# Late nodes of an attention layer as five interleaved generators, with edge pieces at 1.5 a step

## The chip, the core and the metric

The kernel runs on one core of one Trainium2 chip. The metric is the device time of the whole program in microseconds. The core has a tensor engine (PE, whose weight loads the profile shows apart as PEld), a vector engine (DVE), a scalar engine (ACT), GpSimd (POOL), and a queue of its own for plain DMAs (SP). Each engine works through its own list of instructions in order, and semaphores join the lists.

## What is computed

The reference takes 6250 nodes with 128 features and 100000 edges, sorted by destination, and runs four residual blocks of graph layers over them: a mean over neighbours, a product over edges with a radial filter, three layers of neighbour means, and three layers of graph attention. Only the last block matters here. Cut to what is computed, one of its three layers is this:

```python
h = x @ W
al = leaky_relu(h[src] @ a_src + h[dst] @ a_dst + edge_attr @ We @ a_edge, 0.2)   # edges and self loops
ex = exp(al - segment_max(al, dst)[dst])
out = segment_sum(h[src] * ex, dst) / (segment_sum(ex, dst) + 1e-16) + bias
x = batch_norm(leaky_relu(out, 0.01))
```

## The kernel before

The nodes lie in an array of 125 partitions by 50. Each attention layer (`attention_split`) treats them in two parts, in the function `split_edges`, whose instructions are most of the layer's time.

**Early nodes** belong to the first 64 partitions of that array: 3200 nodes, five groups of 128 by 5. For them the gather and the sum are matrix products. A loop of 160 steps, 32 to a group, makes one-hot matrices in each step (`ready`, for the step two ahead: `hot_n` on DVE and ACT, `hot_c` on ACT, from `half_n` and `hot` that SP has loaded), multiplies them on PE into `cnt` (four products), and copies `cnt` to `m` on ACT (L1706). Eight steps make a unit `m`; the next eight steps multiply it with the features on PE (`product`, tile `o`, seven products a step). In the first 128 steps the next group's coefficients are prepared beside that: `source_terms` in the first 20 steps of a group (PE into `x_ps`, DVE from it), and `softmax` in the other 12.

**Late nodes** are the other 3050, 122 partitions by 25 in the code (`R2`, `T2`). Their edges lie in 125 runs of 400. The generator `late` walks all the runs at once, in 50 chunks of 8 edges. A chunk has 8 gathers on POOL into `rows` (three buffers), a short softmax on DVE (`al`, `top`, `ex`) with one exponential on ACT, one product, and 8 dependent accumulations on DVE into `acc` (two buffers), which SP stores to `late_hist` in DRAM. It is cut into four pieces by `yield`. After 200 pieces, `late_fix` repairs sums that cross from one run into another, in seven further pieces, and scatters the result into `late_hist`. Then `late_tail` reads the final sums of the nodes from there, in five blocks of five columns. A block loads the nodes' own rows (`own_h`, by SP), gathers the sums (`agg`, five on POOL), runs through three empty pieces, computes scale factors (`sc`), scales `own_h` on ACT, joins the two on DVE (`stt`, L82), transposes on PE (`tp`), adds the bias on ACT (`z_l`), and gives the activation, the statistics and the copy to `y_t`. `late_tail` runs one block after the other, with eight pieces to a block.

The loop over steps decides how many pieces of `late` each step takes, and this is the order on each engine: at the end of `split_edges` every PE, DVE and ACT instruction is tied to the one recorded before it. POOL and SP are not tied; they run ahead as far as their buffers allow. Before the loop about ten pieces are already done. In the loop:

```python
            while done < min(200, 10 + (step + 1) * 1.38):
                next(edges_late)
                done += 1
            if step > 140:
                for _ in islice(edges_late, 3):
                    pass
```

So the edges end at step 137, the repair begins at step 141 with three pieces a step, and the late nodes follow up to step 157. In a step the pieces stand behind the `m` copy, and ahead of the next step's `cnt`. The helpers `tt`, `ts`, `stt`, `transpose`, `gather`, `scatter` and `bulk` issue one operation each (`bulk` two DMAs); the profile shows their lines (L73, L77, L82, L156, L55, L68, L51 and L52).

Of the kernel before, what the change touches and what calls it, by code (L numbers as in the profile page):

```python
# [39 lines left out]
def kernel(ctx: ExitStack, tc: tile.TileContext, a: dict, out: bass.AP):  # L40
# [7 lines left out]
    def bulk(dst, src, eng=None):  # L48

        eng = eng or nc.sync  # L50
        eng.dma_start(dst[0:PS], src[0:PS])  # L51
        eng.dma_start(dst[PS:], src[PS:])  # L52

    def gather(dst, table, idx):
        nc.gpsimd.indirect_dma_start(  # L55
            out=dst, out_offset=None, in_=table,
            in_offset=bass.IndirectOffsetOnAxis(ap=idx, axis=0))
# [14 lines left out]
    def tt(o, x, y, op):  # L72
        nc.vector.tensor_tensor(o, x, y, op)  # L73

    def ts(o, x, s1, op0, s2=None, op1=None):
        if op1 is None:
            nc.vector.tensor_scalar(o, x, s1, None, op0=op0)  # L77
        else:
            nc.vector.tensor_scalar(o, x, s1, s2, op0=op0, op1=op1)  # L79
# [1058 lines left out]
    def late_nodes(ap, t0, n, width):  # L1138
        return bass.AP(tensor=ap.tensor, offset=ap.offset + (N1 + t0) * width, ap=[[T2 * width, R2], [1, n * width]])
# [311 lines left out]
    def split_edges(lt, i, table, own_d, bias, parts, early_d, late_d, ade, tails, stats, stats_l, pool, ps):  # L1451
# [104 lines left out]
        def late():  # L1556

            NB = 8  # L1560
            top = pool.tile([P, C2 + 1], F32, name="top", bufs=1)
            nc.vector.memset(top[:, 0:1], 0.0)
            prev = None
            for c0 in range(0, C2, NB):
                all_rows = pool.tile([128, NB, W], F32, name="rows", bufs=3)
                for j in range(NB):
                    gather(all_rows[:, j, :], table, lt.src[:, c0 + j:c0 + j + 1])
                rows = all_rows[:P]
                al = pool.tile([P, NB], F32, name="al")
                ex = pool.tile([P, 2, NB], F32, name="ex")  # L1570
                now, before = top[:, c0 + 1:c0 + NB + 1], top[:, c0:c0 + NB]
                tt(al, rows[:, :, AL], ade[:, c0:c0 + NB], OP.add)
                stt(al, al, 0.2, al, OP.mult, OP.max)
                nc.vector.tensor_tensor_scan(now, lt.pen[:, c0:c0 + NB], al, top[:, c0:c0 + 1], op0=OP.add, op1=OP.max)
                tt(ex[:, 0, :], al, now, OP.subtract)
                tt(ex[:, 1, :], before, now, OP.subtract)
                stt(ex[:, 1, :], ex[:, 1, :], 0.0, lt.pen[:, c0:c0 + NB], OP.min, OP.add)
                nc.scalar.activation(ex, ex, AF.Exp)
                yield
                acc = pool.tile([P, NB, W], F32, name="acc")  # L1580
                tt(rows, rows, ex[:, 0, :, None].to_broadcast([P, NB, W]), OP.mult)
                yield
                for j in range(NB):
                    if c0 + j == 0:
                        nc.vector.tensor_copy(acc[:, 0, :], rows[:, 0, :])
                    else:
                        stt(acc[:, j, :], prev, ex[:, 1, j:j + 1], rows[:, j, :], OP.mult, OP.add)
                    prev = acc[:, j, :]
                    if j == NB // 2 - 1:
                        yield  # L1590
                nc.scalar.activation(acc[:, :, AL], now, AF.Copy)
                bulk(bass.AP(tensor=late_hist.tensor, offset=late_hist.offset + c0 * W, ap=[[C2 * W, P], [1, NB * W]]),
                     acc.rearrange("p c f -> p (c f)"))
                yield
            nc.scalar.activation(tails, prev, AF.Copy)
            yield from late_fix(lt, tails, pool, ps)
            yield from late_tail(lt, table, late_d, lt.e_self[i], bias, stats_l, pool, ps)

        def first_terms(al_s):

# [89 lines left out]
        for step in range(steps):  # L1690
            g, s = divmod(step, 32)
            unit, u = divmod(step, 8)
            if s == 0 and g < GP - 1:
                al_s = pool.tile([128, 128], F32, name="al_s")
                terms, soft = source_terms(g + 1, al_s), softmax(g + 1, al_s)
            if u == 0:
                m = pool.tile([128, T, NW, 32], F32, name="m")
            cnt = ps.tile([128, 4, 256], F32, name="cnt", bufs=2)
            hot_n, hot_c = hots.pop(0)
            for w in range(4):  # L1700
                nc.tensor.matmul(cnt[:P, w, :T * NW], lhsT=hot_c[:, w, :P], rhs=hot_n[:, w, :], start=True, stop=True)  # L1701
            if step + 2 < steps:
                hots.append(ready(step + 2))
            for _ in islice(before, 7):
                pass
            nc.scalar.activation(m[:P, :, :, u * 4:u * 4 + 4].rearrange("p l k q -> p k l q"),  # L1706
                                 cnt[:P, :, :T * NW].rearrange("p w (k l) -> p k l w", k=NW), AF.Copy)
            if g < GP - 1:
                if s < 20:
                    for _ in islice(terms, 2 if s % 5 < 3 else 1):  # L1710
                        pass
                else:
                    next(soft, None)
            while done < min(200, 10 + (step + 1) * 1.38):
                next(edges_late)
                done += 1
            if step > 140:
                for _ in islice(edges_late, 3):
                    pass
            if u == 7:  # L1720
                for _ in before:
                    pass
                before = product(unit, m)
# [45 lines left out]
        nc.vector.tensor_copy(fixed[:, AL:AL + 1], mx[:, 1:2])  # L1769
        scatter(late_hist, lt.fix, fixed, P * C2)  # L1770

    def late_tail(lt, table, late_d, e_self, bias, stats_l, pool, ps):

        NK = 5
        for t0 in range(0, T2, NK):
            all_agg = pool.tile([128, NK, W], F32, name="agg", tag="acc")
            agg = all_agg[:R2]
            own_h = pool.tile([R2, NK, W], F32, name="own_h", tag="rows", bufs=3)
            bulk(own_h.rearrange("p t f -> p (t f)"), late_nodes(table, t0, NK, W))
            for j in range(NK):  # L1780
                gather(all_agg[:, j, :], late_hist, lt.end[:, t0 + j:t0 + j + 1])
            for _ in range(3):
                yield
            sc = pool.tile([R2, 6, NK], F32, name="sc")
            own, m = sc[:, 0, :], sc[:, 1, :]
            tt(own, own_h[:, :, AL], late_d[:, t0:t0 + NK], OP.add)
            ts(own, own, e_self[:R2], OP.add)
            stt(own, own, 0.2, own, OP.mult, OP.max)
            tt(m, agg[:, :, AL], own, OP.max)
            tt(sc[:, 2, :], agg[:, :, AL], m, OP.subtract)  # L1790
            tt(sc[:, 3, :], own, m, OP.subtract)
            nc.scalar.activation(sc[:, 2:4, :], sc[:, 2:4, :], AF.Exp)
            yield
            den = sc[:, 4, :]
            tt(den, agg[:, :, ONE], sc[:, 2, :], OP.mult)
            tt(den, den, sc[:, 3, :], OP.add)
            ts(den, den, 1e-16, OP.add)
            nc.vector.reciprocal(den, den)
            tt(sc[:, 2, :], sc[:, 2, :], den, OP.mult)
            tt(sc[:, 3, :], sc[:, 3, :], den, OP.mult)  # L1800
            for j in range(NK):
                nc.scalar.activation(own_h[:, j, :D], own_h[:, j, :D], AF.Copy, scale=sc[:, 3, j:j + 1])  # L1802
            yield
            for j in range(NK):
                stt(agg[:, j, :D], agg[:, j, :D], sc[:, 2, j:j + 1], own_h[:, j, :D], OP.mult, OP.add)
            z = pool.tile([128, NK, R2], F32, name="z_l", tag="wide", bufs=1)
            for j0 in range(0, NK, 2):
                n = min(2, NK - j0)
                tp = ps.tile([128, 2, R2], F32, name="tp", tag="x_ps")
                for j in range(n):  # L1810
                    transpose(tp[:, j, :], agg[:, j0 + j, :D])
                nc.scalar.activation(z[:, j0:j0 + n, :], tp[:, :n, :], AF.Identity, bias=bias, scale=1.0)  # L1812
                if j0 < 4:
                    yield
            stt(z, z, 0.01, z, OP.mult, OP.max)
            for j in range(NK):
                nc.vector.bn_stats(stats_l[:, t0 + j, :], z[:, j, :])
            nc.scalar.activation(lt.y_t.rearrange("f (h c) p -> f c h p", h=2)[:, t0:t0 + NK, :, P1:],
                                 z.rearrange("f c (p h) -> f c h p", h=2), AF.Copy)
            yield  # L1820

    def attention_layers(h_sb, arm=""):
        with tc.tile_pool(name=f"gat{arm}", bufs=1) as gp:
# [310 lines left out]
```

## Time and profile before

| | |
|---|---|
| median of 3 runs | 7095.94 us (7094.98 to 7104.98) |
| profiled execution, its own time | 5981.47 us |
| its span, first to last instruction | 5979.4 us |
| PE / DVE / ACT / POOL busy | 5036.5 / 3978.7 / 3103.4 / 2212.3 us |
| mean granted clock of PE | 0.875 |
| `m<-cnt` of the three layers, first start to last start | 3686.1 to 5917.9 us of the span |

The profiled execution is shorter than the timed runs by 1114 us; both are of the same program. In a waits view a line reads: the engine and line that waited, who released it, the total in us, how often, and the longest. In the stretches view, a row has the stretch and its length in us, then busy us and the number of instructions of each engine, the granted share of PE's clock, the busy share of the DMA engines and their GB/s. In a timeline the first two columns are the start and the duration in us, and brackets hold the idle time ahead and who ended it.

### The profile page before, as it was taken

To read this page: it belongs to the slowest core of one execution; us is meant where nothing else is said; L and a number is where in the kernel's file an instruction comes from. 1 tells how busy PE (TensorE), PEld (TensorE's weight loads), DVE (VectorE), ACT (ScalarE), POOL (GpSimd) and SP (SyncE) were. 2 spreads that over 40 slices of the span, in tenths; PEclk is the share of its full clock that TensorE was granted. 3 is DMA by queue.
4 is the path that set the end of the run, shared out by engine and by line. 5 is a ranking of instruction groups with operands and counts; after the bars stand their busy time and mean duration, and the time that the engine had idled before them with its cause. 6 is when DMAs were issued, how large, how long until landed. Compare 5 with 4: busy or idle time off the path is not lost. (4 is left out here: it accounts for less than half of the span.)

```text
span 5979.4 us, 99205 instructions
## 1 busy us (share of the span) xinstructions
PE 5036.5 (84%) x34468; PEld 3867.5 (65%) x34468; DVE 3978.7 (67%) x12709; ACT 3103.4 (52%) x6518; POOL 2212.3 (37%) x2176
## 2 busy tenths in 40 slices
PE   3289996798888589989979996999869998689996
PEld 3267773344444357766757765888758887578885
DVE  7899985899999641146554226777547775487763
ACT  0166665999999520000000005766747767567674
POOL 0100005777777410010000004666327664276651
PEclk9999996655566589999989997999979999899997
DMA  1123335666666424458888636766447664366652
GB/s 44 29 110 142 147 147 160 189 199 195 194 194 194 137 103 180 188 189 307 309 285 332 246 141 196 207 197 186 119 148 212 204 194 135 126 202 204 192 165 78
DMA packets 403022, 1065.55 MB, mean 178 GB/s; under 512 B 82983, under 2 KB 200395, under 8 KB 383443
## 3 DMA queue, kind: packets, MB, share of 16 engines
q1 hardware_dynamic: 326654, 912.73, 44.7%
q0 software_dynamic: 70080, 143.16, 9.6%
q8 instruction: 273, 4.47, 0.3%
q10 hardware_dynamic: 5772, 3.20, 0.3%
q14 instruction: 243, 1.99, 0.1%
HBM read 752.50 MB, written 306.30 MB: 177 GB/s over the span
## 5 line engine op out<-in xcount | busy, mean ns | idle before, releaser
L55 POOL DMA_INDIRECT rows<-gtable,l_src x1200 | 1209.7, 1008 | 1524.2 <-DMA late_d<-ald 840.9
L887 PEld LDWEIGHTS <-parts 128*128 128x128 bf16 x12000 | 1180.3, 98 | 460.3 <-issue 28.6
L887 PE MATMUL o<-piece,parts 128*128 128x305 bf16 (+1 forms) x9000 | 1253.8, 299 | 30.8 <-ACT parts L869 14.6
L1545 PE MATMUL o<-m,hst 125*128 125x160 f32 x6000 | 919.4, 305 | 102.0 <-ACT m L1706 102.0
L1545 PEld LDWEIGHTS o<-m,hst 125*128 125x128 f32 x6000 | 881.1, 194 | 145.1 <-ACT m L1706 125.3
L1701 PE MATMUL cnt<-hot_n,hot_c 128*125 128x250 f32 x3840 | 938.8, 388 | 13.7 <-ACT m L1706 8.8
L55 POOL DMA_INDIRECT rows<-table,src_all x800 | 815.0, 1019 | 255.9 <-issue 202.8
L1701 PEld LDWEIGHTS cnt<-hot_n,hot_c 128*125 128x125 f32 x3840 | 703.8, 192 | 96.3 <-ACT m L1706 14.9
L1536 ACT ACTIVATE hot_c<-hot,coef_t 128x125 f32<-128x125 bf16 x1920 | 696.7, 388 | 0.4
L904 ACT ACTIVATE h_t<-h_ps 128x500 f32<-128x500 f32 x80 | 34.5, 431 | 964.1 <-PE h_ps L902 833.0
L1706 ACT ACTIVATE m<-cnt 125x1000 f32<-125x1000 f32 x480 | 473.1, 986 | 26.8 <-PE cnt L1701 26.3
L851 ACT ACTIVATE adj<-cnt 128x1000 bf16<-128x1000 f32 x320 | 382.5, 1213 | 183.1 <-PE cnt L849 181.5
L668 PE MATMUL z<-w,s 128*125 128x128 f32 x1600 | 369.0, 402 | 117.4 <-DVE s L82 117.2
L668 PEld LDWEIGHTS z<-w,s 128*125 128x125 f32 x1600 | 316.2, 293 | 222.3 <-DVE s L82 184.5
L887 PE MATMUL o<-adj,parts 128*128 128x320 bf16 (+1 forms) x3000 | 451.8, 297 | 9.4 <-ACT adj L851 8.7
L82 DVE SCALAR_TENSOR_TENSOR acc<-acc,ex,rows 125x130 f32<-125x130 f32 x1197 | 423.1, 353 | 35.0
L659 PE MATMUL z<-bf,w 128*128 128x500 f32 x400 | 369.1, 1023 | 26.0 <-ACT bf L628 25.9
L1535 ACT ACTIVATE hot_n<-half_n 128x250 f32<-128x250 bf16 x960 | 381.8, 398 | 2.4 <-DMA half_n<-node 2.1
L889 DVE COPY agg<-o 128x320 f32<-128x320 f32 x80 | 38.5, 481 | 501.5 <-PE o L887 501.4
L77 DVE TENSOR_SCALAR hot_n<-slots_b,id_t 128x250 bf16<-128x250 bf16 x1250 | 352.1, 282 | 0.0
L77 DVE TENSOR_SCALAR hot_p<-slots_b,hi_t 128x128 bf16<-128x128 bf16 x1250 | 309.6, 248 | 37.4 <-PE cnt L849 37.3
L77 DVE TENSOR_SCALAR hot_n<-l_slot,l_id_t 128x250 f32<-128x250 f32 x960 | 304.6, 360 | 41.1 <-PE cnt L1701 26.2
(489 smaller groups left out, 6788.7 us busy)
## 6 DMA issues: line engine op xcount, KB each, us to landing
piece<-adj SPq DMA_DIRECT2D x60, 2000.0 KB
piece<-adj SPq DMA_DIRECT2D x60, 1906.2 KB
late_hist<-acc SPq DMA_DIRECT2D x150, 455.0 KB
hot<-hot SPq DMA_DIRECT2D x240, 256.0 KB
half_n<-node SPq DMA_DIRECT2D x480, 125.0 KB
dist<-ew_dram SPq DMA_DIRECT2D x50, 1000.0 KB
hot_t<-hot_t SPq DMA_DIRECT2D x192, 256.0 KB
ea<-in_edge_attr SPq DMA_DIRECT2D x100, 448.0 KB
```

Source lines behind the costliest of these rows:

```text
L55: nc.gpsimd.indirect_dma_start(out=dst, out_offset=None, in_=table, in_offset=bass.IndirectOffsetOnAxis(ap=idx, axis=0))
L77: nc.vector.tensor_scalar(o, x, s1, None, op0=op0)
L82: nc.vector.scalar_tensor_tensor(o, x, s, y, op0=op0, op1=op1)
L659: nc.tensor.matmul(z1, lhsT=w1, rhs=bf, start=False, stop=True)
L668: nc.tensor.matmul(z2[:, j, :], lhsT=s1[:, j, :], rhs=w2, start=False, stop=j == HB - 1)
L851: nc.scalar.activation(adj[:, :, :, q - q0:q - q0 + n], cnt[:, :n, :T * NW].rearrange("p w (k l) -> p k l w", k=NW), AF.Copy)
L887: yield nc.tensor.matmul(o[:, :n], lhsT=parts[:, l, s, :], rhs=adj(l), start=(l == 0 and s == 0), stop=(l == T - 1 and s == 2))
L1535: nc.scalar.activation(hot_n[:, w, :], half_n[:, w // 2, :], AF.Copy)
L1536: nc.scalar.activation(hot_c[:, w, :P], lt.hot[:, w0 % WB + w, :P], AF.Copy, scale=coef_t[g][:, w0 + w:w0 + w + 1])
L1545: nc.tensor.matmul(o, lhsT=hst[:, l, :D], rhs=m[:P, l, :], start=(l == 0), stop=(l == T - 1))
L1701: nc.tensor.matmul(cnt[:P, w, :T * NW], lhsT=hot_c[:, w, :P], rhs=hot_n[:, w, :], start=True, stop=True)
L1706: nc.scalar.activation(m[:P, :, :, u * 4:u * 4 + 4].rearrange("p l k q -> p k l q"), cnt[:P, :, :T * NW].rearrange("p w (k l) -> p k l w", ...
```

## The change

`late_tail` becomes a generator for one block (argument `t0`). `late` makes five of them and runs them side by side: every three pieces one more block starts, and in each piece all blocks that have begun run one piece of theirs. A block has ten pieces, one more of them between its `stt` and its transposes, and each pair of transposes is a piece. The edge pieces go at 1.5 a step instead of 1.38, so they end at step 126. From there two pieces a step are run, up to piece 206, and then one. The buffers are divided anew: `agg` takes those of `rows` (three), `own_h` those of `acc` (two), and every second `z_l` has a buffer of its own, where all of them shared the one of `wide`.

```diff
             yield from late_fix(lt, tails, pool, ps)
-            yield from late_tail(lt, table, late_d, lt.e_self[i], bias, stats_l, pool, ps)
+            blocks, running = [late_tail(lt, t0, table, late_d, lt.e_self[i], bias, stats_l, pool, ps)
+                               for t0 in range(0, T2, 5)], []
+            while blocks or running:
+                if blocks:
+                    running.append(blocks.pop(0))
+                for _ in range(3):
+                    running = [b for b in running if next(b, 0) is None]
+                    yield
...
-            while done < min(200, 10 + (step + 1) * 1.38):
+            while done < min(200, 10 + (step + 1) * 1.5):
                 next(edges_late)
                 done += 1
-            if step > 140:
-                for _ in islice(edges_late, 3):
-                    pass
+            if done >= 200:
+                for _ in islice(edges_late, 2 if done < 206 else 1):
+                    done += 1
...
-    def late_tail(lt, table, late_d, e_self, bias, stats_l, pool, ps):
+    def late_tail(lt, t0, table, late_d, e_self, bias, stats_l, pool, ps):
         NK = 5
-        for t0 in range(0, T2, NK):
-            all_agg = pool.tile([128, NK, W], F32, name="agg", tag="acc")
-            own_h = pool.tile([R2, NK, W], F32, name="own_h", tag="rows", bufs=3)
+        all_agg = pool.tile([128, NK, W], F32, name="agg", tag="rows", bufs=3)
+        own_h = pool.tile([R2, NK, W], F32, name="own_h", tag="acc")
...
         for j in range(NK):
             stt(agg[:, j, :D], agg[:, j, :D], sc[:, 2, j:j + 1], own_h[:, j, :D], OP.mult, OP.add)
-            z = pool.tile([128, NK, R2], F32, name="z_l", tag="wide", bufs=1)
+        yield
+        z = pool.tile([128, NK, R2], F32, name="z_l", tag="wide" if t0 % 10 else "z_l", bufs=1)
         for j0 in range(0, NK, 2):
...
             nc.scalar.activation(z[:, j0:j0 + n, :], tp[:, :n, :], AF.Identity, bias=bias, scale=1.0)
-                if j0 < 4:
-                    yield
+            yield
```

More of the change, by code (lines that the diff above doesn't have):

```diff
@@ L1770, in late_fix @@
         scatter(late_hist, lt.fix, fixed, P * C2)
-    def late_tail(lt, table, late_d, e_self, bias, stats_l, pool, ps):
+    def late_tail(lt, t0, table, late_d, e_self, bias, stats_l, pool, ps):
         NK = 5
-        for t0 in range(0, T2, NK):
-            all_agg = pool.tile([128, NK, W], F32, name="agg", tag="acc")
-            agg = all_agg[:R2]
-            own_h = pool.tile([R2, NK, W], F32, name="own_h", tag="rows", bufs=3)
[L1779 to L1782, printed above, removed]
-                yield
[L1784 to L1792, printed above, removed]
-            yield
[L1794 to L1802, printed above, removed]
-            yield
-            for j in range(NK):
-                stt(agg[:, j, :D], agg[:, j, :D], sc[:, 2, j:j + 1], own_h[:, j, :D], OP.mult, OP.add)
-            z = pool.tile([128, NK, R2], F32, name="z_l", tag="wide", bufs=1)
[L1807 to L1812, printed above, removed]
-                if j0 < 4:
[L1814 to L1820, printed above, removed]
@@ new lines, in late_tail @@
+        all_agg = pool.tile([128, NK, W], F32, name="agg", tag="rows", bufs=3)
+        agg = all_agg[:R2]
+        own_h = pool.tile([R2, NK, W], F32, name="own_h", tag="acc")
+        bulk(own_h.rearrange("p t f -> p (t f)"), late_nodes(table, t0, NK, W))
+        for j in range(NK):
+            gather(all_agg[:, j, :], late_hist, lt.end[:, t0 + j:t0 + j + 1])
+        for _ in range(3):
+            yield
+        sc = pool.tile([R2, 6, NK], F32, name="sc")
+        own, m = sc[:, 0, :], sc[:, 1, :]
@@ new lines, in late_tail @@
+        tt(own, own_h[:, :, AL], late_d[:, t0:t0 + NK], OP.add)
+        ts(own, own, e_self[:R2], OP.add)
+        stt(own, own, 0.2, own, OP.mult, OP.max)
+        tt(m, agg[:, :, AL], own, OP.max)
+        tt(sc[:, 2, :], agg[:, :, AL], m, OP.subtract)
+        tt(sc[:, 3, :], own, m, OP.subtract)
+        nc.scalar.activation(sc[:, 2:4, :], sc[:, 2:4, :], AF.Exp)
+        yield
+        den = sc[:, 4, :]
+        tt(den, agg[:, :, ONE], sc[:, 2, :], OP.mult)
+        tt(den, den, sc[:, 3, :], OP.add)
@@ new lines, in late_tail @@
+        ts(den, den, 1e-16, OP.add)
+        nc.vector.reciprocal(den, den)
+        tt(sc[:, 2, :], sc[:, 2, :], den, OP.mult)
+        tt(sc[:, 3, :], sc[:, 3, :], den, OP.mult)
+        for j in range(NK):
+            nc.scalar.activation(own_h[:, j, :D], own_h[:, j, :D], AF.Copy, scale=sc[:, 3, j:j + 1])
+        yield
+        for j in range(NK):
+            stt(agg[:, j, :D], agg[:, j, :D], sc[:, 2, j:j + 1], own_h[:, j, :D], OP.mult, OP.add)
+        yield
+        z = pool.tile([128, NK, R2], F32, name="z_l", tag="wide" if t0 % 10 else "z_l", bufs=1)
@@ new lines, in late_tail @@
+        for j0 in range(0, NK, 2):
+            n = min(2, NK - j0)
+            tp = ps.tile([128, 2, R2], F32, name="tp", tag="x_ps")
+            for j in range(n):
+                transpose(tp[:, j, :], agg[:, j0 + j, :D])
+            nc.scalar.activation(z[:, j0:j0 + n, :], tp[:, :n, :], AF.Identity, bias=bias, scale=1.0)
+            yield
+        stt(z, z, 0.01, z, OP.mult, OP.max)
+        for j in range(NK):
+            nc.vector.bn_stats(stats_l[:, t0 + j, :], z[:, j, :])
+        nc.scalar.activation(lt.y_t.rearrange("f (h c) p -> f c h p", h=2)[:, t0:t0 + NK, :, P1:],
+                             z.rearrange("f c (p h) -> f c h p", h=2), AF.Copy)
@@ L1822, in attention_layers @@
+        yield
     def attention_layers(h_sb, arm=""):
```

## The prediction

> **What bounds the kernel now.** I read the page first, for the engines and the span.
>
> ```profile
> span 5979.4 us, 99205 instructions
> PE 5036.5 (84%) x34468; PEld 3867.5 (65%) x34468; DVE 3978.7 (67%) x12709; ACT 3103.4 (52%) x6518; POOL 2212.3 (37%) x2176
> ```
>
> The busy shares are averages over unlike stages, and the diff touches attention alone, so I cut its third layer by the ends of `m<-cnt` (L1706 runs once a step) and asked for the stretches: steps 1 to 127 (edges beside the next group's source terms and softmax), 128 to 139 (edges alone), 140 to 143 (repair of the late sums), 144 to 159 (late nodes).
>
> ```profile
> core 0: us, PE busy (x) PEld busy (x) DVE busy (x) ACT busy (x) POOL busy (x), PEclk, DMA share, GB/s
> 5246.00:5772.20 526.20, 484.03 (x4038) 446.58 (x4035) 408.48 (x1191) 365.51 (x1019) 362.59 (x356) 0.97 0.67 197
> 5772.20:5812.20 40.00, 39.50 (x239) 36.99 (x240) 24.54 (x79) 34.00 (x95) 13.30 (x13) 1.00 0.59 174
> 5812.20:5828.10 15.90, 15.75 (x95) 14.43 (x93) 4.08 (x17) 12.11 (x35) 1.28 (x1) 1.00 0.31 89
> 5828.10:5918.90 90.80, 64.45 (x345) 56.20 (x345) 35.87 (x150) 58.67 (x155) 25.46 (x26) 0.87 0.21 59
> ```
>
> By step these are 526.2/127 = 4.14 us, 40.0/12 = 3.33, 15.9/4 = 3.98 and 90.8/16 = 5.68. In the second stretch PE is busy 39.5 of 40.0: 3.33 us is the floor PE sets for a step, edges included. In the last, PE is idle 26 us. It costs 90.8 - 16 x 3.33 = 37.5 us over the floor; layers 1 and 2 show 89.9 and 90.0 us by the same marks. What PE waits for there is in the waits of that stretch:
>
> ```profile
> PE tp L156 <- DVE agg L82: 14.9, 5, 10.5
> PE tp L156 <- ACT z_l L1812: 8.9, 7, 3.2
> PE o L1545 <- ACT m L1706: 0.6, 2, 0.4
> ```
>
> All 23.8 us are the late nodes' transposes `tp`. The timeline shows the largest: the repair's scatter, the first block's gather that must follow it, the arithmetic that needs all five gathers, and PE at the end of it.
>
> ```profile
> 5829.46 1.31 POOL L68 DMA_INDIRECT late_hist<-fixed,l_fix  x1 [12.28 <-DVE fixed L1769]
> 5833.82 0.97 POOL L55 DMA_INDIRECT agg<-late_hist,l_end  x1 [3.04 <-issue]
> 5838.86 0.95 POOL L55 DMA_INDIRECT agg<-late_hist,l_end  x1 [0.30 <-issue]
> 5841.68 0.36 DVE L73 TENSOR_TENSOR sc<-agg,sc 122x5 f32<-122x5 f32 x2 [11.47 <-DMA agg<-late_hist,l_end]
> 5844.44 0.76 PE L156 MATMUL tp<-ident,agg 122*128 122x122 f32 x2 [10.53 <-DVE agg L82]
> ```
>
> With three pieces in a step, a block's three empty pieces are one step, 3 to 4 us, but the gathers need 5841.68 - 5829.46 = 12.2 us from the scatter's start. Of the 37.5 us, 23.8 are these waits, 7.6 the 25 transposes themselves (mean 351 ns), and about 6 the slower clock after the long gap (share granted 0.87).
>
> **What the Trainium skill says.** "TensorE: Matmul & The Clock Gate", section "Part 1: The HAM clock gate (the "warmup" mystery)", says that PE falls to half rate after an idle window of about 3.4 us. The trace agrees: after the 10.5 us gap the stretch 5848.1 to 5865.2 has a granted share of 0.81, the others around it 0.97 and 1.00. "DMA: Bandwidth & Descriptors", section "Anatomy of one DMA — SWDGE (gpsimd) path", gives about 2.0 us fixed for one DMA. The trace has 5841.68 - 5839.81 = 1.9 us from the end of the fifth gather's issue to its first reader, so the chain can't be made shorter, only covered.
>
> **The change, part by part.**
>
> *Late nodes side by side.* No instruction of the five blocks goes away; the built order keeps 25 transposes, scalings and gathers a layer, but one piece of each live block runs in a step. The waits' fate: after the scatter three whole steps pass before `sc`, at 3.4 to 3.9 us 10 to 12 us against 12.2, so DVE may be late by 0 to 2 us, which `hot_n` and `hot_c`, made two steps ahead, cover. The `stt` of a block and its transposes are now a step apart, as are the transposes and the `z_l` copies: the 23.8 us should go, and with the gap the half clock. What is late next is ACT. Its 144-to-159 stretch has 25 `own_h` at 392 ns, 15 `z_l` at 428, 5 `y_t` at 765: 7.8 + 6.4 + 3.8 + 1.0 = 19 us for blocks now spread over 23 steps (pieces 208 to 229 of the generator, steps 130 to 152). ACT without them is busy 34.0/12 = 2.83 us a step, with them 2.83 + 19/23 = 3.66; PE is 3.33 + 7.6/23 = 3.66. Two engines equally full, in a lumpy order (five `own_h` and a `z_l` fall in one step of three), never fit perfectly. I take an excess of 15 us a layer over the floor: 7.6 that must be, and as much again lost. Bounds: 8 (perfect fit) to 27 (ACT waits for `tp` at the end of most steps). Gain 37.5 - 15 = 22 us a layer, 10 to 29.
>
> *The repair.* 15.9 us for four steps is 2.6 over the floor. At two pieces a step instead of three it has fewer waits in a step, but starts beside the last chunk's store, which its gather must follow. Left at 0, -1 to +2.
>
> *Queues.* On SP, `own_h` moves from three buffers to two: block k+2's load waits for the `stt` of block k, one step earlier, and the next `half_n` loads stand behind it. `half_n` is loaded about two steps (7 us) ahead and waited for 0.7 us in 526; cover gone, it would cost up to 1 us a block. On POOL, `agg` has three buffers instead of two, so three blocks gather in a row, 15 x 1.25 = 19 us, where three of five waited for transposes before; nothing else is queued on POOL then. The separate `z_l` buffer only removes a wait. I take 0 for all, -1 to +3 a layer.
>
> *Edge pieces at 1.5.* By step 127 the old pace has done 10 + 128 x 1.38 = 187 pieces, the new one 200: 13 pieces, 3.25 chunks, move into the stretch with source terms, and leave steps 128 to 137, where they were free (3.33 us either way). A chunk's DVE work is 8 x 354 + 1242 + 235 + 5 x 168 ns = 5.15 us, so 16.7 us of DVE move. DVE idles 118 us in the stretch, 61 of them waiting for PE, so part of it disappears. But ACT, in order, waits there for DVE's edge pieces:
>
> ```profile
> ACT acc L1591 <- DVE acc L82: 115.3, 40, 5.7
> ACT ex L1578 <- DVE ex L82: 32.4, 30, 2.7
> PE o L1545 <- ACT m L1706: 30.3, 15, 3.8
> ```
>
> Busy plus these waits is 366 + 148 = 514 of 526 us, and PE pays at each unit's start. I take half of the moved DVE time: +8 us a layer, 0 to +21 (all of it and 1.3 us of ACT per chunk). POOL's cover: a gather starts every 1.25 us, a chunk needs 10.1 to 10.5, and a chunk's period goes from 4/1.38 x 4.14 = 12.0 to 11.0 us. It still keeps up, at 94%, with a lead (from a chunk's last gather to the `al` that reads it, in the timeline) of 5 us at the start of a layer and about 15 later.
>
> **Sum.** -22 + 8 = -14 us a layer, -42 for three. The profiled execution took 5981.47 us by its own clock (2 us outside the span) and would take 5939. The median of the runs is 7095.94, 1114 us more; no view shows why. I carry the difference over unscaled: 7054. If the runs are longer because PE is slower in them, the edges get cheaper and the tail's waits shorter alike, and the sum moves little.
>
> **The rivals.**
>
> *Slower: the edge pace costs more than the tail gives.* A unit of 8 steps carries 12 pieces instead of 11. If each added piece delays the unit's last `m` in full, that is 1.29 us of DVE and 0.8 of ACT, 2.1 a unit, 33 a layer for 16 units; less 22, +11, so +33: 7129. For it: ACT's 514 of 526 us. Against: DVE's 61 us of waiting for PE, and the PE-bound steps. It decides once steps 0 to 127 take over 4.14 + 22/127 = 4.31 us.
>
> *The tail becomes ACT's.* If ACT waits for `tp` at the end of each step, the excess stays at 27; -10 + 8 = -2 a layer, so 7090. For it: ACT and PE both at 3.66.
>
> *The edges are free.* With the tail at 10 over the floor, -27 a layer: 7015. For it: 3.33 us with edges beside.
>
> *The change doesn't do what it says*: in the timed runs PE may be so slow that the waits are already hidden; then 7096.
>
> **How the numbers follow.** A measurement can tell about 0.2%, 14 us. Likeliest case (-42, its own range -20 to -66) 0.50; edges free 0.20; ACT's tail 0.13, half of it over 14 us faster; nothing 0.06; slower 0.11. So faster 0.77, same 0.12, slower 0.11. The range, 7008 to 7100, leaves out the slower case and the far end of the free one.
>
> **What would show it.** Right: in the profile after, the last 34 steps of a layer without a PE gap over 3 us, `tp` waiting under 8 us a layer, no half-clock stretch after the scatter, and steps 130 to 152 at 3.8 to 4.1 us; steps 1 to 127 at 4.15 to 4.25. Wrong: `rows` gathers ending waits of `al`, steps 1 to 127 at 4.31 or more, or steps 130 to 152 above 4.5 with ACT full.

## The result, and the profile after

Timed in one comparison, the kernel before took 7098.29 us (median of 22 runs) and the changed kernel 7077.39 (22 runs): ratio 0.9971, interval 0.9960 to 0.9981, 20.9 us faster. The forecast was 42 faster. The sign and the range hold; half the gain is missing. The experiments show that the late nodes gave more than forecast, and that one term took much of it back: on chips like those of the timed runs a term of the forecast that was put at nothing, the run of gathers, and on the faster kind the pace of the edge pieces.

First the changed kernel's page: its first lines.

```profile
span 7065.9 us, 99076 instructions
...
PE 5341.6 (76%) x34468; PEld 4038.6 (57%) x34468; DVE 3967.9 (56%) x12709; ACT 3112.6 (44%) x6518; POOL 2184.3 (31%) x2176
```

This execution took 7067.68 us by its own time, in line with its timed runs, while the profile of before on which the forecast rests took 5981.47. So these two profiles can't be laid side by side. The kernel before was profiled again (run b_again, 7084.81 us, on chip A of the table below). The stretches view of the third layer, cut at the same steps as in the forecast (the first row is steps 1 to 127, the second steps 128 to 139, the last one steps 144 to 159), for before in that usual execution:

```profile
core 0: us, PE busy (x) PEld busy (x) DVE busy (x) ACT busy (x) POOL busy (x), PEclk, DMA share, GB/s
6113.50:6872.00 758.50, 577.57 (x4040) 504.31 (x4038) 407.18 (x1194) 370.30 (x1018) 362.17 (x361) 0.85 0.50 138
6872.00:6914.50 42.50, 40.94 (x240) 37.92 (x241) 24.12 (x79) 33.63 (x94) 7.56 (x8) 0.98 0.53 153
...
6930.30:7022.90 92.60, 65.46 (x345) 57.06 (x345) 35.82 (x150) 58.92 (x156) 25.23 (x26) 0.85 0.22 58
```

and for the changed kernel (steps 1 to 127, 128 to 139, 140 to 143, 144 to 159):

```profile
6120.30:6876.70 756.40, 570.90 (x4040) 499.13 (x4038) 423.84 (x1248) 370.96 (x1026) 373.33 (x370) 0.86 0.51 142
6876.70:6931.50 54.80, 47.95 (x255) 41.85 (x256) 18.23 (x78) 37.30 (x104) 18.97 (x20) 0.88 0.35 89
6931.50:6948.70 17.20, 15.42 (x92) 13.92 (x90) 9.14 (x43) 15.91 (x45) 7.02 (x8) 1.00 0.49 130
6948.70:7005.50 56.80, 54.30 (x331) 50.80 (x331) 19.38 (x73) 48.09 (x126) 0.00 (x0) 1.00 0.19 52
```

Two things stand out. Steps 144 to 159 went from 92.6 to 56.8 us with PE busy 54.3 of them: the waits for `tp` are gone. And steps 128 to 139 took 54.8 us where 42.5 were enough before, with PE idle almost 7 us. Step 133 alone took 17.2 us (15.5 and 17.0 in the other layers). The timeline of POOL, then of PE, for that time:

```profile
6883.73 1.24 POOL L68 DMA_INDIRECT late_hist<-fixed,l_fix  x1 [6.34 <-DVE fixed L1777]
6887.47 0.97 POOL L55 DMA_INDIRECT agg<-late_hist,l_end  x1 [2.51 <-DMA late_hist<-fixed,l_fix]
6888.74 0.95 POOL L55 DMA_INDIRECT agg<-late_hist,l_end  x1 [0.30 <-issue]
...
6904.98 0.94 POOL L55 DMA_INDIRECT agg<-late_hist,l_end  x1 [0.30 <-issue]
6928.03 0.94 POOL L55 DMA_INDIRECT agg<-late_hist,l_end  x1 [22.11 <-PE tp L156]
```

```profile
6897.05 0.85 PE L1709 MATMUL cnt<-hot_n,hot_c 128*125 128x250 f32 x2
6898.25 0.47 PE L1709 MATMUL cnt<-hot_n,hot_c 128*125 128x250 f32 x1 [0.35 <-issue]
6899.66 0.37 PE L1709 MATMUL cnt<-hot_n,hot_c 128*125 128x250 f32 x1 [0.93 <-issue]
...
6908.90 1.43 PE L1545 MATMUL o<-m,hst 125*128 125x160 f32 x4 [0.28 <-issue]
```

Fifteen gathers, 1.25 us apart, fill POOL from 6887.5 to 6905.9. From 6897.05 to 6908.90 PE starts 14 instructions, one per 0.9 us on average, with gaps of mostly 0.2 to 0.9 us that the profile puts down to nothing it sees ("issue"); in the steps ahead of it a whole step with its 22 records takes 3.6 us. ACT and DVE stand still in the same time; the waits view of the last 32 steps has them as "remote", a releaser that it can't name:

```profile
ACT m L1714 <- remote: 14.4, 1, 14.4
...
DVE hot_n L77 <- remote: 13.2, 1, 13.2
```

In the loop over the edges of this kernel and of b_again the same two labels are all over, and there POOL gathers most of the time. Of the 1103 us by which b_again's span is longer than the first profile's, 706 lie there (235 us a layer in steps 1 to 127), and 352 ahead of attention, which begins at 4038 us of the span in place of 3686.

### The profile page after: what moved, and what is told of

It reads as the page before. It is cut to its first block, busy times and chain, and to the rows that moved or that the text cites. A ratio compares the mean times of both kernels' runs of the same rounds, so it can differ in the third digit from the quotient of the medians.

```text
span 7065.9 us, 99076 instructions
## 1 busy us (share of the span) xinstructions
PE 5341.6 (76%) x34468; PEld 4038.6 (57%) x34468; DVE 3967.9 (56%) x12709; ACT 3112.6 (44%) x6518; POOL 2184.3 (31%) x2176
## 5 line engine op out<-in xcount | busy, mean ns | idle before, releaser
L1545 PE MATMUL o<-m,hst 125*128 125x160 f32 x6000 | 1059.6, 327 | 346.3 <-issue 265.5
L1545 PEld LDWEIGHTS o<-m,hst 125*128 125x128 f32 x6000 | 981.4, 211 | 438.1 <-issue 328.8
L1709 PE MATMUL cnt<-hot_n,hot_c 128*125 128x250 f32 x3840 | 1052.5, 413 | 157.2 <-issue 122.3
L55 POOL DMA_INDIRECT rows<-table,src_all x800 | 789.8, 987 | 608.8 <-DVE run L79 338.9
L1709 PEld LDWEIGHTS cnt<-hot_n,hot_c 128*125 128x125 f32 x3840 | 753.1, 206 | 298.6 <-issue 178.0
L659 PE MATMUL z<-bf,w 128*128 128x500 f32 x400 | 388.6, 1075 | 301.0 <-ACT bf L628 218.6
L73 DVE TENSOR_TENSOR one<-x_ps,col 128x400 f32<-128x400 f32 x192 | 109.6, 571 | 652.9 <-remote 399.5
L628 ACT ACTIVATE soft<-z 128x500 f32<-128x500 f32 (+1 forms) x400 | 231.2, 578 | 412.6 <-remote 244.6
```

The source lines that it names most:

```text
L55: nc.gpsimd.indirect_dma_start(out=dst, out_offset=None, in_=table, in_offset=bass.IndirectOffsetOnAxis(ap=idx, axis=0))
L659: nc.tensor.matmul(z1, lhsT=w1, rhs=bf, start=False, stop=True)
L1545: nc.tensor.matmul(o, lhsT=hst[:, l, :D], rhs=m[:P, l, :], start=(l == 0), stop=(l == T - 1))
```

## The experiments

The kernels were run in batches, each on one chip; the five batches fell on five chips, here A to E. For the result itself and the first profile the chip isn't known. The kernel before took about 7086 us on A, 6986 on C, and 5986, 5988 and 5978 on B, D and E. Ratios are to the runs of before on the same chip. Step sums are means over the three layers of the profiled execution, from the end of one `m` copy to another.

| run | chip | time, us | ratio, interval | steps 1-127 | steps 128-159 | step 133 |
|---|---|---|---|---|---|---|
| before, first profile | not known | 5981.5 | - | 523.9 | 146.1 | 3.6 |
| b_again | A | 7084.8 | - | 759.1 | 150.1 | 2.7 |
| after, profile | not known | 7067.7 | 0.9971, 0.9960-0.9981 | 768.6 | 128.2 | 16.6 |
| e_pace | A | 7107.1 | 1.0028, 1.0015-1.0040 | 763.6 | 148.2 | 3.6 |
| e_tail138 | A | 7053.8 | 0.9949, 0.9931-0.9967 | 759.9 | 136.8 | 2.8 |
| e_spaced | A | 7018.9 | 0.9907, 0.9886-0.9928 | 767.5 | 116.0 | 3.6 |
| e_spaced138 | B | 5911.2 | 0.9880, 0.9859-0.9900 | 523.5 | 118.6 | 3.6 |
| e_ten | B | 5966.0 | 0.9966, 0.9953-0.9979 | 548.9 | 115.1 | 3.6 |
| e_plain | B | 5997.5 | one run | 529.4 | 145.5 | 3.6 |
| e_tied | B | 5962.9 | 0.9961, 0.9949-0.9973 | 532.3 | 120.2 | 3.6 |
| after_2 | C | 6926.6 | 0.9920, 0.9899-0.9942 | 740.2 | 126.6 | 14.1 |
| e_tail138_2 | C | 6953.0 | 0.9944, 0.9922-0.9966 | 735.1 | 132.5 | 2.7 |
| e_spaced138_2 | C | 6895.8 | 0.9859, 0.9832-0.9886 | 734.6 | 123.2 | 2.7 |
| e_plain_2 | C | 6291.1 | one run | 527.8 | 147.3 | 3.6 |
| after_3 | D | 5960.1 | 0.9967, 0.9953-0.9982 | 548.5 | 115.0 | 3.6 |
| e_ten_2 | D | 5966.2 | 0.9967, 0.9954-0.9979 | 546.5 | 115.1 | 3.6 |
| e_pace_2 | D | 6049.4 | 1.0108, 1.0092-1.0125 | 547.0 | 144.8 | 3.6 |
| e_spaced_2 | D | 5964.1 | 0.9965, 0.9951-0.9979 | 547.7 | 115.1 | 3.6 |
| e_ten_3 | E | 5963.1 | 0.9973, 0.9961-0.9984 | 550.4 | 115.0 | 3.6 |
| e_tied_2 | E | 5961.9 | 0.9971, 0.9958-0.9983 | 530.6 | 119.7 | 3.6 |

On A and C the three layers of one profile differ by up to 19 us in steps 1 to 127, so there the ratios decide; on B, D and E the step sums of kernels with the same loop repeat within 4 us.

**b_again: the kernel before, unedited.**

> The kernel before, profiled once more, since its first profiled execution was 1114 us shorter than its median. Theory (the first profile shows an unusual execution): this one takes about 7098 us by its own clock, a layer's steps 1 to 127 last 750 to 780 us as in the profile of the changed kernel (there 756 to 775) instead of 523 to 526, with PE waits put down to issue, and steps 128 to 159 stay at about 146 us. Rival (the profiling of the changed kernel was the unusual one): 5981 us and 525 us again.

It took 7084.81 us; steps 1 to 127 took 759 us a layer where the first profile showed 524, and steps 128 to 159 took 150, near the expected 146. The first profile was of another kind of execution than the timed runs.

**e_pace: the pace alone.**

```diff
 (kernel before)
-            while done < min(200, 10 + (step + 1) * 1.38):
+            while done < min(200, 10 + (step + 1) * 1.5):
```

> The kernel before with the edge pieces at 1.5 a step and nothing else. The prediction's term: +8 us a layer (0 to 21), so +24, about 7122 us. Rival: in the executions that are timed the edge stretch is set by PE's own waits (issue), so the moved pieces cost nothing: 7098 us. The slower rival of the prediction: +33 a layer, 7197 us.

20.9 us slower by the medians, 6.6 a layer by the ratio (3.5 to 9.4 by its interval): on chip A the forecast's pace term holds.

**e_tail138: the tail alone.**

```diff
 (changed kernel)
-            while done < min(200, 10 + (step + 1) * 1.5):
+            while done < min(200, 10 + (step + 1) * 1.38):
```

> The changed kernel with the old pace of 1.38, so that the five generators start at step 137 and their last pieces run after the loop. If the pace costs 8 us a layer, this is 24 us below the changed kernel less some 5 us for the pieces behind the loop: about 7058 us. If the pace is free: 7077 to 7085 us.

Ratio 0.9949, 36 us below before. With the pace's 20 us that leaves 16 us for both edits of the changed kernel on A, near the 20.9 measured. The slow stretch moves with the scatter: in this kernel step 143 takes 16 to 18 us and step 133 under 3.

**e_spaced: the gathers of each block tied to its step.** A small memset on DVE, which has its place in the order of the loop, writes the tile that the gathers fill, so that a block's five gathers start no earlier than that memset.

```diff
 (changed kernel, in late_tail)
         all_agg = pool.tile([128, NK, W], F32, name="agg", tag="rows", bufs=3)
+        nc.vector.memset(all_agg[:, :, 0:1], 0.0)
```

> The changed kernel with one small DVE memset of agg ahead of each block's gathers, so that POOL can't gather three blocks in a row (15 gathers, 19 us) but goes block by block with the steps. Theory: in the changed kernel's profile PE stumbles for 12 us a layer (6897 to 6909) in that long run of gathers, and m takes 15 to 17 us at step 133; with the runs broken the stumble goes, -10 us a layer or about 7047 us. Rival: the stumble comes with the scatter and the first block whatever follows: step 133 stays at 15 us and the time at 7077 us.

Ratio 0.9907. Against the changed kernel's 0.9971 this is 0.0064 of 7090 us: 45 us, 15 a layer. The two ratios are of different batches, since the changed kernel wasn't run on A; by the step sums of the two profiles it is 12 a layer. The timeline of POOL in layer 3 has groups of five with a pause between:

```profile
6851.35 0.94 POOL L55 DMA_INDIRECT agg<-late_hist,l_end  x1 [0.30 <-issue]
6854.98 1.05 POOL L55 DMA_INDIRECT agg<-late_hist,l_end  x1 [2.69 <-DVE hot_n L77]
...
6860.09 0.95 POOL L55 DMA_INDIRECT agg<-late_hist,l_end  x1 [0.30 <-issue]
6866.94 1.05 POOL L55 DMA_INDIRECT agg<-late_hist,l_end  x1 [5.90 <-DVE hot_n L77]
```

Step 133 is back at 3.6 us, and steps 128 to 159 fall from 128.2 to 116.0. The same 25 gathers a layer, spaced, show no slow stretch. So on this kind of chip the fifteen in a row bring it about.

**e_spaced138: both edits together.** (`e_spaced` with the pace at 1.38.)

> The side-by-side tail with its gathers tied to their steps (as in the run e_spaced) and the edge pieces back at 1.38 a step. Theory, that the three terms add up (tail side by side, gathers in a row, pace): the pace was worth +21 us alone, the run of gathers -46 us in the ratio, so the ratio is about 0.9907 - 0.003 = 0.988, some 84 us below the kernel before; steps 1-127 of a layer as before (755 to 765 us), steps 128-159 about 121 us. Rival, that the faster pace pays back in the tail what it costs in the loop: the ratio stays at 0.990 or above.

0.9880 on B, the number expected, but by luck: the sum was made for a chip with slow stretches and 760 us for steps 1 to 127, and B has neither (523.5 us, before 5986 us in all). So it was repeated on the other kind: e_spaced138_2, below.

**e_ten: ten gathers in a row.**

```diff
 (changed kernel, in late_tail)
+        if t0 >= 2 * NK:
+            nc.vector.memset(all_agg[:, :, 0:1], 0.0)
```

> The changed kernel, with only the third to fifth block's gathers tied to their steps: after each scatter ten gathers run in a row instead of fifteen (or, in e_spaced, five). Theory, that TensorE, ScalarE and VectorE stumble only from about 11 us into an unbroken run of gathers: ten gathers last 10 x 1.25 = 12.5 us, so the stumble is 0 to 3 us, step 133 (m to m) takes 3.6 to 7 us instead of 15.5 to 17.2, and the ratio is 0.990 to 0.993. Rival, that any gathers issued straight after the scatter cost their share: a third less than with fifteen, step 133 at 10 to 13 us and the ratio near 0.995.

Step 133 took 3.6 us, but on this chip nothing shows a slow stretch, so this tells neither theory. What it told was unexpected: steps 1 to 127 took 549 us where the first profile of before shows 524 and e_spaced138, at the old pace, 523.5.

**e_plain: the gathers of the edges left out.**

```diff
 (kernel before, in late)
-                for j in range(NB):
-                    gather(all_rows[:, j, :], table, lt.src[:, c0 + j:c0 + j + 1])
                 rows = all_rows[:P]
+                bulk(rows.rearrange("p c f -> p (c f)"), nodes(table, c0 % 40, NB, W))
```

> The kernel before, with the eight gathers of each edge chunk (GpSimd's indirect DMAs) replaced by one plain load of eight blocks of consecutive rows of the same table on SP's queue; it leaves out the gathering of the edges' rows, so its values of the edges are not the reference's. Bytes moved into SBUF and all arithmetic stay. Theory, that the slow pace of steps 1-127 belongs to GpSimd's gathers: steps 1-127 fall from about 760 to 525 us a layer or less, and the total falls to about 7090 - 3 x 235 = 6385 us or below (the filter stage gathers too). Rival, that it belongs to the amount of DMA traffic or to TensorE's own rate: steps 1-127 stay at about 760 us and the total above 7000.

5997 us on B in its one run, where before takes 5986: there leaving the gathers out saves nothing.

**e_tied: the edge gathers in pairs, two chunks ahead.**

```diff
 (e_spaced138, in late)
+            ahead = []
+            def fetch(c0, part):
+                ...
+                new, j0 = ahead[-1], part * (NB // 4)
+                nc.vector.memset(new[:, j0:j0 + NB // 4, 0:1], 0.0)
+                for j in range(j0, j0 + NB // 4):
+                    gather(new[:, j, :], table, lt.src[:, c0 + j:c0 + j + 1])
...
-                for j in range(NB):
-                    gather(all_rows[:, j, :], table, lt.src[:, c0 + j:c0 + j + 1])
+                rows = ahead.pop(0)[:P]
+                fetch(c0 + 2 * NB, 0)
```

(and parts 1 to 3 after the next three pieces.)

> As e_spaced138, with the gathers of the edge chunks spread too: each chunk's rows are gathered two chunks ahead, two gathers after each of the four pieces of a chunk, each pair held back by a small memset on VectorE so that no eight run in a row. Theory, that long unbroken runs of gathers make the other engines stumble and short ones don't: steps 1-127 fall from about 760 us a layer towards 525, and the total lies up to 3 x 235 us below e_spaced138. Rival, that the stumble in these steps depends on the number of gathers and not on their grouping (POOL is busy with them most of the time either way): steps 1-127 stay within 750 to 790 us and the total within 0.5% of e_spaced138, or above it by the 4 memsets a chunk.

52 us slower than e_spaced138 on B: 8.8 us a layer in steps 1 to 127, 1.6 in the later ones, and some 22 us in all between the layers. Where gathers don't disturb, tying them only costs. What it does on the other kind of chip wasn't seen.

**Chip C: after_2, e_tail138_2, e_spaced138_2, e_plain_2** (the kernels of those names, on another chip).

> The changed kernel itself, once more. So far there are two groups of executions of the kernel before, one near 7090 us and one near 5985 us, each on another chip. Theory, that the chip decides whether TensorE, ScalarE and VectorE slow down beside gathers: where before takes about 5985 us, the changed kernel shows no slow stretch after the scatter (step 133 at 3.6 us) and its gain is that of the run e_ten (ratio 0.9955 to 0.9975); where before takes about 7090 us, the ratio is again 0.996 to 0.998 and step 133 takes 15 to 17 us. Rival, that the slow stretch is the kernel's own and shows on both: step 133 at 15 us or more on either chip, and the ratio near 1.003 on the faster one.

> The changed kernel with the edge pieces at 1.38 a step, once more. Theory, that the pace of 1.5 costs more where the step itself is short: on a chip where before takes about 5985 us, steps 1-127 of a layer go back from about 549 us to 523 us and the ratio is 0.986 to 0.990; on one where before takes about 7090 us, 0.995 as before. Rival, that the pace costs the same 21 us on both: ratio 0.993 on the faster chip.

> The side-by-side tail with spaced gathers and pace 1.38, once more, beside e_tail138 in the same call: on a chip where before takes about 5985 us both theories of the slow stretch after the scatter give the two kernels apart by at most 0.2% if there is no slow stretch there; on one where before takes about 7090 us, spacing is worth about 45 us again and the ratio is 0.988 to 0.990.

> The kernel before without the gathers of the edges (one plain load in the place of the eight), once more; it leaves out the gathering of the edges' rows. On a chip where before takes about 5985 us it was 5997 us, so gathers cost nothing there. On one where before takes about 7090 us: theory, that the slow pace of steps 1-127 belongs to the gathers: about 525 us a layer in place of 760 and a total near 6400 us or below; rival, that it belongs to DMA traffic of any kind or to the chip as a whole: about 760 us and above 7000 us.

C is of the slower kind, and step 133 of after_2 took 14.0, 15.5 and 12.7 us. Its ratio, 0.9920, is below the expected 0.996 to 0.998: here the changed kernel gained 56 us, where the timed comparison shows 20.9. Why, no run shows; before wasn't profiled on C. Spacing the gathers (e_spaced138_2 against e_tail138_2, in one batch) was worth 57 us, 19 a layer, of which the profiles show 9 in steps 128 to 159. The decisive run is e_plain_2: 6291 us in place of 6986. Its stretches view for steps 1 to 127 of layer 3:

```profile
5552.30:6080.20 527.90, 483.25 (x4038) 446.16 (x4036) 400.63 (x1192) 365.88 (x1019) 0.00 (x0) 0.97 0.67 197
```

With no gather on POOL in the loop and as many bytes a second as in the first profile of before (197 GB/s), the loop on C is as fast as on B: 527.8 us a layer against 529.4. So the slow loop on C comes from the gathers, and not from the amount of DMA traffic or a slower PE; for A the same is likely but wasn't tried. What of a gather does it (POOL's own work, the queue of its DMAs, or their packets) this run can't tell, since all three go together. The stages before attention, which this kernel leaves as they were, still end late: attention starts at 3985 us on C against 3692 on B, and these 293 us are the whole difference of the two runs (6291 and 5997).

The pace can't be read on C: after_2 at 1.5 and e_tail138_2 at 1.38 have overlapping intervals.

**Chip D: after_3, e_ten_2, e_pace_2, e_spaced_2.**

> The changed kernel, beside e_ten_2 and e_pace_2 of the same call. If before takes about 5985 us here: theory, no slow stretch after the scatter (step 133 at 3.6 us), steps 1-127 at about 549 us a layer, ratio 0.9955 to 0.9975 as in e_ten; rival, the forecast's own sum holds, steps 1-127 at about 531 us and the ratio near 0.993. If before takes 6950 us or more: step 133 at 13 to 17 us again, ratio 0.991 to 0.998.

> Ten gathers in a row after the scatter in place of fifteen. Where before takes 6950 us or more: theory, the slow stretch begins about 11 us into an unbroken run, so ten gathers (12.5 us) show 0 to 3 us of it and step 133 takes 3.6 to 7 us, near e_spaced_2; rival, each gather costs its share, step 133 at 10 to 13 us and the time two thirds of the way from e_spaced_2 to after_3. Where before takes about 5985 us: the same as after_3 within 0.2%.

> The kernel before with the pace of 1.5 alone. Where before takes about 5985 us: theory, 25 us a layer in steps 1-127 and part of it back in the late steps, ratio 1.005 to 1.013; rival, the forecast's 8 us a layer, ratio 1.003 to 1.005. Where before takes 6950 us or more: ratio 1.001 to 1.004 as in e_pace.

> The changed kernel with the gathers of each block tied to its step. Where before takes about 5985 us: theory, the same as after_3 within 0.3%, as there is no slow stretch to take away. Where before takes 6950 us or more: step 133 at 3.6 us, 0.4 to 0.7% below after_3; rival, that the faster time of e_spaced was a matter of that one call, no difference.

D is of the faster kind, that of the forecast's profile, so here the forecast's sum can be judged by its own terms. There is no slow stretch: spacing makes no difference (0.9967 and 0.9965). Yet the changed kernel gains only 19.8 us by its ratio. The stretches view of after_3, layer 3, beside the one in the forecast:

```profile
5236.50:5784.60 548.10, 492.05 (x4036) 455.99 (x4032) 424.24 (x1245) 366.89 (x1025) 379.01 (x370) 0.95 0.68 196
5784.60:5826.80 42.20, 41.46 (x255) 38.97 (x256) 18.63 (x78) 37.56 (x105) 19.34 (x20) 1.00 0.43 116
5826.80:5842.80 16.00, 15.17 (x91) 13.86 (x89) 9.04 (x42) 15.50 (x44) 7.13 (x8) 1.00 0.48 134
5842.80:5899.70 56.90, 54.30 (x331) 50.79 (x331) 19.43 (x74) 48.27 (x127) 0.00 (x0) 1.00 0.19 53
```

The tail is all that it could be: PE busy 54.3 of 56.9 us at full clock. The loop over steps 1 to 127 took 548.1 us against 526.2. e_pace_2 shows that this is the pace alone: 1.0108, 64.7 us, 21.6 a layer, with 547.9 us in the same stretch. The waits view of that stretch of e_pace_2:

```profile
ACT acc L1591 <- DVE acc L82: 130.2, 44, 6.0
...
PE o L1545 <- ACT m L1706: 45.3, 15, 4.2
...
POOL rows L55 <- DVE acc L82: 21.1, 9, 4.2
```

PE's wait for `m` at the start of the fifteen units rose from 30.3 to 45.3 us, one microsecond a unit, with ACT's wait for DVE's `acc` up from 115.3 to 130.2. Other waits of PE fell a little, so its idle time grew by 12.2 us (42.2 to 54.4). PE itself was busy 493.5 us in place of 484.0 with nearly the same number of matmuls, at a granted share of 0.95 instead of 0.97:

```profile
5292.40:5840.30 547.90, 493.54 (x4042) 456.96 (x4040) 424.87 (x1247) 366.85 (x1026) 380.12 (x369) 0.95 0.69 197
```

Together 12.2 + 9.5 = 21.7, which is what the stretch grew by (547.9 - 526.2). DVE waits for gathers of `rows` 1.0 us in all, so POOL isn't the cause. The Trainium skill, "TensorE: Matmul & The Clock Gate", section "Part 1: The HAM clock gate (the "warmup" mystery)", puts the idle window that halves PE's rate at about 3.4 us. The timeline of PE, two waits of e_pace_2 and then one of the first profile of before, agrees only in part:

```profile
5362.19 2.17 PE L1545 MATMUL o<-m,hst 125*128 125x160 f32 x14 [3.66 <-ACT m L1706]
...
5396.08 4.10 PE L1545 MATMUL o<-m,hst 125*128 125x160 f32 x14 [4.20 <-ACT m L1706]
```

```profile
5406.21 2.86 PE L1545 MATMUL o<-m,hst 125*128 125x160 f32 x14 [2.16 <-ACT m L1706]
```

After the 4.20 us wait the fourteen records of `o` took 4.10 us, after one of 3.66 us the usual 2.17. But after only 2.16 us they took 2.86, and the granted share from 5407.5 to 5410.9 was 0.51. So the length of one wait doesn't decide by itself. In the stretch, e_pace_2 has 13 gaps of PE over 2 us and 11 stretches at half clock, 54 us in all; before has 7 and 7, 27 us in all.

**Chip E: e_ten_3, e_tied_2.**

> Ten gathers in a row after the scatter in place of fifteen. Where before takes 6950 us or more: theory, the slow stretch begins about 11 us into an unbroken run, so ten gathers (12.5 us) show 0 to 3 us of it and step 133 takes 3.6 to 7 us, the ratio 0.5% below that of the changed kernel on such a chip; rival, each gather costs its share, step 133 at 10 to 13 us. Where before takes about 5985 us: step 133 at 3.6 us and 0.9967 again, which tells neither.

> The spaced tail at pace 1.38 with the edge gathers issued in pairs, two chunks ahead. Where before takes 6950 us or more: theory, only long unbroken runs of gathers slow the other engines, and steps 1-127 fall from 735 to 765 us a layer towards 530, the total to about 6400; rival, their number decides, and steps 1-127 stay within 720 to 790 us. Where before takes about 5985 us: 0.996 again, which tells neither.

E is of the faster kind too. Both repeat what B and D showed, and tell nothing on the length of the run of gathers.

**What is settled, and what not.** e_spaced138 is faster than the kernel before on both kinds of chip, 0.988 on B and 0.986 on C, and than the changed kernel, which has 0.992 on C and 0.997 on D (it wasn't run on B). Not settled: whether the slow stretch depends on the length of an unbroken run of gathers (in the profile after it begins about 10 us after the first of them) or on their density; what in the chip or its setting makes the two kinds; by what path a gather on POOL delays the other engines, and whether it delays ACT and DVE itself or only through PE, whose `cnt` they wait for; and why the changed kernel gained 56 us on C and 20.9 in the timed runs. The difference went with the batch and so with the chip; that it is the chip and nothing else of the batch isn't shown.

## Why the prediction was half right

*Bound and mechanism: right on D.* No `tp` wait is left, on either kind. On D no PE gap over 3 us remains in the last 34 steps, none runs at half clock, and steps 130 to 152 take 3.69 us in layer 3, a little under the 3.8 to 4.1 foreseen. In the profile of the changed kernel the slow stretch spoils two of these signs: half clock after the scatter (a share of 0.88 in steps 128 to 139) and 4.29 us for steps 130 to 152. On the clock, the "0.97 and 1.00" that the forecast sets against 0.81 are the earlier rows of its table; right behind, 5865.2 to 5918.9, the share was 0.94.

*Late nodes side by side: right, undersized.* Forecast -22 us a layer (10 to 29). On D steps 128 to 159 fell by 146.1 - 115.0 = 31.1. The excess over the floor, put at 15 with a lower bound of 8, is 115.0 - 32 x 3.33 = 8.4: the perfect fit that I had said a lumpy order never reaches. In steps 140 to 143 ACT is busy 15.5 and PE 15.2 of 16.0 us, both nearly full, but the excess of 8.4 is far from the 27 of the rival of ACT's tail, which falls. On A, e_spaced shows 150.1 - 116.0 = 34, from one profile each.

*Queues: this step failed, for the measured time.* "... three blocks gather in a row, 15 x 1.25 = 19 us ... nothing else is queued on POOL then. ... I take 0 for all." The 19 us are right, and nothing is queued behind them; but on chips like A and C, where the timed runs belong, PE slows and ACT and DVE stand still beside the run of gathers, whose queue they do not share. It cost 12 to 15 us a layer by e_spaced, 9 to 19 by the pair on C (the lower numbers by step sums, the higher by ratios). The bound of +3 looked only at who waits in POOL's queue.

*Edge pieces at 1.5: right on A, wrong on the kind of chip that it was worked out from.* Forecast +8 a layer (0 to 21). On A 6.6. On D 21.6 by the times, 23 to 25 by steps 1 to 127. The step that failed there is "half of the moved DVE time". ACT's and PE's waits each grew by 15 us, nearly all of the 16.7 us of DVE work that moved, where half was taken, and the 9.5 us of longer PE busy time at a lower clock were not in the sum. That is most of the way to the mechanism of the first rival (33 a layer), whose point of 4.31 us a step was reached: 548.5/127 = 4.32. The total did not turn slower, since the tail gave 31 and not 22. On A a step of the loop takes 6.0 us, and a chunk's period 4/1.5 x 6.0 = 16 us. That the added pieces find room there, in time that is lost anyway, is argued and not shown.

*Edges free:* excluded on D by e_pace_2, on A by e_pace.

*The sum.* On D: -31 + 24.6 = -6.5 a layer, -19.5 in all; measured -19.8. On A, e_tail138 has the late nodes side by side with the run of gathers, -12 a layer; with e_pace's 6.6 that is -5.4, -16 in all; measured -20.9. Of the -12, the run of gathers is 12 to 15, so the late nodes alone are -24 to -27, against the 34 of single profiles; these sizes are rough. So the timed gain is nearly that of D for another reason, and the forecast of -14 a layer was wrong in both. On C the gain was 19 a layer, and which term differs there is open.

*The 1114 us.* "No view shows why" was true of that profile; carrying them over unscaled gave nearly the right total by luck and was wrong for the terms. "The edges get cheaper and the tail's waits shorter alike" is half right: the edges did (6.6 in place of 21.6), the tail's waits did not (92.6 against 90.8 us in steps 144 to 159).

## What to carry to other kernels

Before making a sum, see that the profiled execution's own time agrees with the timed runs; if it doesn't, profile again, since a term can be three times as large in one kind of execution as in the other (the pace: 21.6 and 6.6 us a layer). When an edit lets gathers on POOL run ahead unhindered, give the run a price for the other engines too (here 0 on one kind of chip, 9 to 19 us for fifteen gathers on the other), and where the gathers aren't needed early, tie them to the step that uses them. And where one engine waits in order for another's pieces, work moved into that stretch can count nearly in full, as on D, with a slower clock after many of the longer waits on top.

## What the runs showed of the hardware that was not expected

The same program took 5978 to 5988 us on three chips and 6986 and 7086 on two others, repeatably within a batch. With the edge gathers left out, attention took 2243 us from the first to the last `m` copy on C and 2242 on B, while the kernel before took 2232 in the first profile and 2984 on A. Beside the gathers of a long run PE started an instruction every 0.9 us on average, for 12 us, with nothing that the profile shows to wait for. And a wait of PE of 2.16 us was followed by a stretch at half clock, while one of 3.66 us was not.
